# Layer 1's queries and values as 15 block products per half of the tokens, in a two-layer attention kernel

## The chip, the cores and the metric

The kernel runs on one core of a Trainium2 chip. Its time is the device time of one execution in microseconds (us), and the time before is the median of three executions. One further execution was taken with the hardware profiler; the profile's rows and the trace come from it. The engines are TensorE (PE in the profile; its weight loads are PEld), VectorE (DVE), ScalarE (ACT), GpSimd (POOL) and SyncE (SP). Each takes the instructions of its own queue in order. SP issues most transfers, POOL and ScalarE issue some.

## What is computed

Eight images of 32 x 32 = 1024 tokens with 384 channels go through two layers in float32. Layer 0 is group norm, attention with 6 heads and relative positions, and a projection, added to the input. Layer 1 is attention with one causal head of 384 channels, added to its input; a feed-forward block with binarized weights follows it. Cut to what matters here:

```python
def _L1_attn_ref(x, Wq, Wk, Wv):
    q = jnp.einsum('btc,ch->bth', x, Wq)
    k = jnp.einsum('btc,ch->bth', x, Wk)
    v = jnp.einsum('btc,ch->bth', x, Wv)
    scores = jnp.einsum('bth,bsh->bts', q, k) * scale
    ...
    return jnp.einsum('bts,bsh->bth', softmax(scores), v)

x = x + _L0_conv_ref(_gn(x), ...)
t = _to_tokens(x)
t = t + _L1_attn_ref(_ln_t(t), L1_attn_Wq, L1_attn_Wk, L1_attn_Wv)
t = t + _L1_ffn_ref(_ln_t(t), L1_ffn_W1, L1_ffn_b1, L1_ffn_W2, L1_ffn_b2)
```

The feed-forward block's output is zero for all but the first five images, so the kernel leaves it out for images 5, 6 and 7.

## The kernel before

The images are worked one after the other, in the order 5, 0, 1, 2, 3, 4, 6, 7 (`ORDER`). A tile is at most 128 partitions wide; the 384 channels are three blocks of 128. Tiles are taken from pools of buffers: 12 pages of 128 x 1024, 10 larger `image` (or `flat`) buffers, and the 8 banks of PSUM, which `o_tile` hands out. A scheduler orders the instructions of each engine when the program is built; `tc.issue_after(ins)`, and `behind_of`, which calls it, put the instructions that the block creates on `ins`'s engine behind `ins` in that engine's queue. `last_ended` is the VectorE instruction that such a block last stood behind, `in_turn` does the same for TensorE.

Layer 0 (`layer0`, `attend0_fast`) makes queries by plain products (L629), and keys and values by a scheme that was there before (L555): the three input blocks and the three output blocks of the weights, with the 1024 tokens in two halves of 512, make a product of a 2 x 3 by a 3 x 3 block matrix, which takes 18 block products plainly and 15 by this scheme. The scheme works on forms: sums and differences of the input's blocks (`image_forms`, L527) and of the weights' blocks (`weight_forms`, L172, made once by POOL into `wf`). `PROD_ORDER` (L40) lists the 15 products with the PSUM bank (A to F) in which each accumulates and the name under which ScalarE copies the bank's running value to SBUF (`keep`, L581). Between some copies VectorE takes differences (`PROD_COMBINE`, L606), and it ends each of the six output blocks with one sum of a bank and a kept value (`finish`, L614; the order that comes out is D, E, F, C, B, A). A bank that is copied midway takes further products after the copy.

In the scores loop of layer 0 a pair of heads p and a half of the queries take 16 us; VectorE adds up the probabilities (L862) and POOL multiplies the output by the reciprocals (L912). During pair 1 the tables `r` of the last pair are placed by 16 transfers, 8 issued by SP and 8 by POOL (`place`, L743), and `residual` (L820) loads the input again and adds a bias on POOL (L823).

Layer 1 (`attention1`, L981) begins with the projection of layer 0's output (L472, `more`), layer norm of the first half of the tokens (`layer_norm_T`: statistics, normalising to xn at L462, transposing by TensorE at L398 and copying to lnT by ScalarE at L399), and goes on with queries (L989) and values (L472, copied at L993) for each half of 512 tokens. The keys are not made: scores are formed with the product of Wq and Wk^T, which `multiply_out` (L378) computes once and keeps in SBUF as `wqk`. Then `between` runs the group norm of the next image (`group_norm_T`, L411): VectorE takes statistics (L418) and aggregates them (L419), TensorE averages over the groups with a one-column product (L422), VectorE goes on with the mean (L424 to L427), and a second such product follows (L430). The scores of layer 1 (L1030), their exponentials (L1039) and the values (L1045) stand behind it in `attend1_fast`. At the very start, `turn_biases` (L164) transposes bias rows on TensorE, VectorE copies the result (L167), and `join_biases` (L362) multiplies part of it on TensorE.

Of the kernel before, what the change touches and what calls it, by code (L numbers as in the profile page):

```python
# [11 lines left out]
F32 = mybir.dt.float32  # L12
# [7 lines left out]
P = 128  # L20
# [71 lines left out]
def conv_attn_hybrid(  # L92
# [35 lines left out]
    wproj_sb, wv_sb = (tile_of(n, [P, NC, C]) for n in ("wproj_sb", "wv_sb"))  # L128
# [11 lines left out]
    def load_weights(pools):  # L140
# [16 lines left out]
        nc.sync.dma_start(out=wv_sb, in_=wv.rearrange("(k p) o -> p k o", p=P))  # L157
# [6 lines left out]
    def turn_biases(pools, rows):  # L164
        ps = pools.o_tile("biases")
        nc.tensor.transpose(ps[:, : 3 * NC + NM], rows, ident[: 3 * NC + NM, : 3 * NC + NM])
        nc.vector.tensor_copy(biases, ps[:, : 3 * NC + NM])  # L167
# [4 lines left out]
    def weight_forms(pools, eng, raw, s):  # L172
# [3 lines left out]
        room = pools.page(f"wsum_{s}")  # L176
# [5 lines left out]
        def f(r):  # L182
            return wf[:, r, s - 1, :]
# [101 lines left out]
    w2s = store.tile([P, NM * C], F32R, name="w2s")  # L285

    def load_plain():
        nc.sync.dma_start(out=wqkv_sb, in_=qkv_w.rearrange("(p k) o -> p k o", k=NC))
    wqk = const.tile([P, NC, C], F32, name="wqk")
# [88 lines left out]
    def multiply_out(pools, wqT_sb, wkT_sb):  # L378

        for m in range(NC):  # L380
# [5 lines left out]
            with tc.issue_after(first_root[0]):  # L386
                nc.scalar.mul(wqk[:, m, :], ps[:, :C], C**-0.5)

    def stages(pools):
# [137 lines left out]
        def image_forms(b, xT, eng):  # L527

            rooms = [pools.page(f"xf_{b}_{i}") for i in range(len(X_MADE) // 2)]
            made = {r: rooms[i // 2][:, ts(i % 2, 512)] for i, r in enumerate(X_MADE)}  # L530

            def x(k, n):
                return xT[:, k, ts(n, 512)]

            def add(r, a, b, op=ALU.add):
                eng.tensor_tensor(made[r], a, b, op)  # L536
# [17 lines left out]

        class ProductSet:  # L555

            def __init__(self, b, s, forms):
                self.name, self.s, self.forms = f"{b}_{s}", s, forms
# [4 lines left out]
            def kept(self, name):  # L563
                if name not in self.part:
                    pair = next(pair for pair in PROD_PAGES if name in pair)
                    room = pools.page(f"u_{self.name}_{pair[0]}")
                    self.part.update({n: room[:, ts(i, 512)] for i, n in enumerate(pair)})
                return self.part[name]

            def multiply(self, ps, r, start):  # L570
                x, w = self.forms[r], wf[:, r, self.s - 1, :]
                if self.s == 1:
                    in_turn(ps, w, x, start=start, stop=True, skip_group_check=True)
                    return
                keys = x.rearrange("p (g i n) -> p g n i", g=2, n=2)
                for j in range(4):
                    in_turn(
                        ps[:, ts(j, P)], keys[:, j // 2, j % 2], w, start=start and j == 0, stop=True, skip_group_check=True
                    )
# [779 lines left out]
```

## Time and profile before

| what | us |
|---|---|
| executions, median of three (lowest to highest) | 2315.85 (2315.0 to 2317.25) |
| the profiled execution | 2316.79 |
| its span, from the first to the last instruction | 2314.8 |
| TensorE busy | 2295.1 |
| layer 1's queries, L989, 18 matmuls per image | 127.5 busy |
| layer 1's values, L472, 24 matmuls per image | 126.5 busy |
| VectorE, ScalarE, POOL busy | 1526.6, 1099.2, 413.4 |

The profiled execution is one execution, 0.9 us above the median. The mean granted clock of TensorE was 0.998 of full speed over the span. A matmul in float32 leaves two records in the profile, so "x12" stands for six matmuls; its records overlap with those of the next one, so that the distance from start to start, and not the duration of one record, is what it costs. "Idle before" is the time in which an engine had nothing to do just before an instruction, with what ended it behind the arrow. A line number is that of the helper that creates the instruction: L525 holds layer 0's queries, position tables and block products alike, and L472 both the projection of layer 0 and the values of layer 1. Three rows by form, for the operations that the change multiplies: line, engine, operation, tiles, shapes and count; busy time and mean duration; idle time before.

```
L606 DVE TENSOR_TENSOR f_u_n<-f_u_n,f_u_m 128x512 f32<-128x512 f32 x32 | 22.1, 691 | 17.4
L586 ACT COPY f_u_n<-f_pr_A 128x512 f32<-128x512 f32 x48 | 28.2, 587 | 42.6
L536 POOL TENSOR_TENSOR f_xf<-f_gnT 128x512 f32<-128x512 f32 x28 | 35.5, 1279 | 503.0
```

### The profile page before, as it was taken

To read this page: it belongs to the slowest core of one execution; us is meant where nothing else is said; L and a number is where in the kernel's file an instruction comes from. 1 tells how busy PE (TensorE), PEld (TensorE's weight loads), DVE (VectorE), ACT (ScalarE), POOL (GpSimd) and SP (SyncE) were. 2 spreads that over 40 slices of the span, in tenths; PEclk is the share of its full clock that TensorE was granted. 3 is DMA by queue.
4 is the path that set the end of the run, shared out by engine and by line. 5 is a ranking of instruction groups with operands and counts; after the bars stand their busy time and mean duration, and the time that the engine had idled before them with its cause. 6 is when DMAs were issued, how large, how long until landed. Compare 5 with 4: busy or idle time off the path is not lost.

```text
span 2314.8 us, 27729 instructions
## 1 busy us (share of the span) xinstructions
PE 2295.1 (99%) x9971; PEld 1317.8 (57%) x9971; DVE 1526.6 (66%) x2432; ACT 1099.2 (47%) x1876; POOL 413.4 (18%) x520
## 2 busy tenths in 40 slices
PE   8999999999999999999999999999999999999998
PEld 4545554568645577545685455874457754555454
DVE  5885578575887348884468864579734788527851
ACT  4642266137663257642467522766324765116611
POOL 4320222030140201311102302013020131021300
PEclk9999999999999999999999999999999999999999
DMA  6530561040730115510318102074002362017100
GB/s 164 155 116 1 152 139 56 38 162 28 148 99 28 62 48 119 129 54 1 110 40 187 47 28 109 28 142 105 28 28 82 97 140 64 1 51 159 37 1 29
DMA packets 153980, 185.82 MB, mean 80 GB/s; under 512 B 110901, under 2 KB 123562, under 8 KB 151018
## 3 DMA queue, kind: packets, MB, share of 16 engines
q1 hardware_dynamic: 135456, 113.28, 20.2%
q0 software_dynamic: 17184, 69.22, 9.5%
q8 instruction: 82, 1.34, 0.2%
q10 hardware_dynamic: 1194, 1.45, 0.2%
q14 instruction: 64, 0.52, 0.1%
HBM read 83.24 MB, written 50.33 MB: 58 GB/s over the span
## 4 chain that ended last, share of the span: by engine, by line
PE 97%; DVE 1%; ACT 1%; DMA 0%; issue 0%; POOL 0%; ACTq 0%; DVEq 0%
PE f_s L844 15%; PE f_av L870 14%; PE f_s L1030 8%; PE f_av L1045 8%; PE f_y L1155 7%; PE f_y L1205 7%; PE f_pj L472 5%; PE f_v L472 5%; PE f_q L989 5%; PE f_qk L525 5%; PE f_pr_A L525 4%; PE f_s L848 4%; PE f_pr_B L525 3%; PE f_rel L525 2%; PE f_pt L398 1%; PE f_pr_D L525 1%
## 5 line engine op out<-in xcount | busy, mean ns | idle before, releaser
L855 ACT ACTIVATE f_pr<-f_s 128x512 f32<-128x512 f32 x768 | 413.2, 595 | 41.2 <-PE f_s L848 34.7
L844 PE MATMUL f_s<-f_q,f_k 64*128 64x512 f32 x1536 | 399.0, 595 | 0.0
L862 DVE TENSOR_TENSOR f_sum<-f_sum,f_pr 128x1024 f32<-128x1024 f32 x288 | 363.3, 1262 | 23.5 <-ACT f_pr L855 1.4
L870 PE MATMUL f_av<-f_pr,f_v 128*64 128x512 f32 x1536 | 339.3, 594 | 0.0
L848 PE MATMUL f_s<-f_r,unit 64*128 64x512 f32 x768 | 307.4, 792 | 0.0
L870 PEld LDWEIGHTS f_av<-f_pr,f_v 128*64 128x64 f32 x1536 | 106.2, 137 | 196.4 <-issue 191.9
L844 PEld LDWEIGHTS f_s<-f_q,f_k 64*128 64x128 f32 x1536 | 145.6, 186 | 124.0 <-issue 64.6
L1030 PE MATMUL f_s<-f_q,f_lnT 128*128 128x512 f32 (+3 forms) x576 | 195.9, 488 | 0.0
L1045 PE MATMUL f_av<-f_v,f_pr 128*128 128x385 f32 x576 | 195.3, 486 | 0.0
L1039 ACT ACTIVATE f_pr<-f_s 128x512 f32<-128x512 f32 (+3 forms) x96 | 46.9, 491 | 279.6 <-DVE f_s L1035 233.9
L743 POOL DMA_DIRECT2D f_r<-f_far x192 | 102.2, 535 | 401.2 <-DVE f_far L737 189.5
L1045 PEld LDWEIGHTS f_av<-f_v,f_pr 128*128 128x128 f32 x576 | 108.2, 190 | 77.2 <-issue 11.5
L1030 PEld LDWEIGHTS f_s<-f_q,f_lnT 128*128 128x128 f32 x576 | 102.0, 190 | 77.8 <-issue 53.8
L1166 DVE TENSOR_REDUCE am<-f_h 128x1 f32<-128x1024 f32 (+2 forms) x80 | 71.6, 947 | 96.3 <-ACT f_h L1159 96.3
L1159 ACT ACTIVATE f_h<-f_y,biases 128x256 f32<-128x256 f32 x240 | 100.9, 472 | 67.4 <-PE f_y L1155 67.4
L525 PE MATMUL f_qk<-f_gnT,wq_sb 128*128 128x512 f32 x288 | 127.8, 595 | 0.0
L989 PE MATMUL f_q<-f_lnT,wqk 128*128 128x512 f32 x288 | 127.5, 592 | 0.0
L472 PE MATMUL f_pj<-wproj_sb,f_oT 128*128 128x384 f32 x384 | 127.3, 488 | 0.0
L1205 PE MATMUL f_y<-f_w2a,f_hilo 128*128 128x384 f32 x640 | 127.1, 341 | 0.2
L472 PE MATMUL f_v<-wv_sb,f_lnT 128*128 128x384 f32 x384 | 126.5, 486 | 0.0
L848 PEld LDWEIGHTS f_s<-f_r,unit 64*128 64x128 f32 x768 | 75.0, 187 | 90.0 <-issue 89.8
L536 POOL TENSOR_TENSOR f_xf<-f_gnT 128x512 f32<-128x512 f32 x28 | 35.5, 1279 | 503.0 <-DVE f_gnT L435 503.0
(217 smaller groups left out, 3519.2 us busy)
## 6 DMA issues: line engine op xcount, KB each, us to landing
f_far<-f_far SPq DMA_DIRECT2D x48, 512.0 KB, 4.6
f_r<-f_far SPq DMA_DIRECT2D x192, 128.0 KB, 2.9
f_r<-f_far POOLq DMA_DIRECT2D x192, 128.0 KB, 4.5
f_far<-f_far SPq DMA_DIRECT2D x192, 64.0 KB, 4.7
f_x<-in_x SPq DMA_DIRECT2D x32, 384.0 KB, 7.2
f_gnT<-in_xT SPq DMA_DIRECT2D x21, 512.0 KB, 4.5
f_w1a<-w1s POOLq DMA_DIRECT2D x5, 1536.0 KB, 6.8
f_w2a<-w2s POOLq DMA_DIRECT2D x5, 1536.0 KB, 9.2
```

The costliest lines, as they stand in the source:

```text
L472: nc.tensor.matmul(ps[:, :C], xT[:, k, ts(j, P)], w[:, k, cols], start=(k == 0), stop=(k == NC - 1))
L525: last_product[0] = nc.tensor.matmul(*args, **kw).ins
L844: nc.tensor.matmul(sc[par], k[rows[par], p, ts(c, P)], q[rows[par], p, ts(half, 512)], start=True, stop=False)
L848: last_matmul[0] = nc.tensor.matmul(sc[par], unit[rows[par], c // 2 % 2].rearrange("i h w -> i (h w)"), r(2 * (c // 4) + c % 2, p)[rows[pa ...
L855: last_exp[0] = nc.scalar.activation(pr[:, ts(par, 512)], sc[par], AF.Exp).ins
L862: adds.append(nc.vector.tensor_tensor(total, total, pr, ALU.add).ins)
L870: last_matmul[0] = nc.tensor.matmul(av[ts(par, HD), :], v[:, c, ts(2 * p + par, HD)], pr[:, ts(par, 512)], start=(c == 0), stop=(c == NJ - 1),
L989: nc.tensor.matmul(ps, wqk[:, k, ts(m, P)], xT[:, half, k, :], start=(k == 0), stop=(k == NC - 1))
L1030: nc.tensor.matmul(sc[:, lo:], xT[:, c // 4, k, ts(c % 4, P)], q[:, half, k, lo:], start=(k == 0), stop=(k == NC - 1),)
L1045: nc.tensor.matmul(av[:, : C + 1], prs[c][:, ts(j - c, P)], v[:, c, :], start=(c == 0), stop=(c == j))
L1155: nc.tensor.matmul(ps, w1k[i // 2][:, ts(m, P)], xs[i % 2][:, half, i // 2, :], start=(i == 0), stop=(i == 2 * NC - 1))
L1205: nc.tensor.matmul(ps[:, :C], h, w, start=(i == 0), stop=(i == len(products) - 1))
```

## The change

The queries and the values of layer 1 are made by the same 15-product scheme, once per half of the tokens, with the half's 512 tokens in two blocks of 256. A set of products is thus 15 matmuls of 256 columns for queries, and 15 x 2 matmuls of 128 tokens by 128 channels for values; there are four sets per image.

- `sum_forms` generalises `image_forms` to a width and to an engine for each form. In layer 1, POOL makes forms 5, 6 and 12 and VectorE the others, from lnT.
- `ProductSet` takes the weights' forms, a width, the token tiles, whether a bias is added, and the engine of the differences, which is POOL for the sets of layer 1. The ten copies by ScalarE and the six final sums by VectorE (to q and v) are as in layer 0.
- The queries of half 0 come ahead of the layer norm of half 1, then the forms of half 1, the values of half 0, and the queries and values of half 1.
- The weights' forms of layer 1, `w1f`, are made once by POOL, in the first image (image 5), after `residual`: 42 operations on 128 x 128 blocks. For this `wqk` is written to memory by SP at the start and read back with Wv (SP also) at that time. SP no longer loads Wv at the start. `w1f` takes the place of `wqk` and `wv_sb` in SBUF.
- The group norm of the next image is put behind the last final sum (`behind_of(last_ended[0])`).
- ScalarE in place of VectorE copies the transposed biases.

The core of the diff:

```diff
-        nc.vector.tensor_copy(biases, ps[:, : 3 * NC + NM])
+        nc.scalar.copy(biases, ps[:, : 3 * NC + NM])
...
+    def layer1_forms(pools):
+        room = pools.flat("raw_1")
+        plain = [room[:, ts(i, NC * C)] for i in range(2)]
+        nc.sync.dma_start(out=plain[0], in_=wqk_kept)
+        nc.sync.dma_start(out=plain[1].rearrange("p (k o) -> p k o", k=NC), in_=wv.rearrange("(k p) o -> p k o", p=P))
+        for s in range(2):
+            weight_forms(pools, nc.gpsimd, plain[s].rearrange("p (k o) -> p k o", k=NC), s, w1f)
...
-                nc.scalar.mul(wqk[:, m, :], ps[:, :C], C**-0.5)
+                nc.scalar.mul(made[:, m, :], ps[:, :C], C**-0.5)
+        nc.sync.dma_start(out=wqk_kept, in_=made.rearrange("p k c -> p (k c)"))
...
+                            made = self.eng.tensor_tensor(self.part[dst], self.part[dst], self.part[other], ALU.subtract)
+                        if self.eng is nc.vector:
+                            last_ended[0] = made.ins
...
                 if (p, half) == (1, 0):
                     xt = residual()
+                    if b == ORDER[0]:
+                        layer1_forms(pools)
...
+            def forms_of(half):
+                return sum_forms(
+                    f"1_{b}_{half}", lambda k, n: xT[:, half, k, ts(n, 256)], 256,
+                    lambda r: nc.gpsimd if r in (5, 6, 12) else nc.vector,
+                )
+
+            def products(half, forms):
+
+                def put_queries(ps, kept, p, n, op):
+                    return nc.vector.tensor_tensor(q[:, half, p, ts(n, 256)], ps, kept, op).ins
+
+                def put_values(ps, kept, p, n, op):
+                    ps, kept = (t.rearrange("t (j c) -> t j c", j=2) for t in (ps, kept))
+                    j = 4 * half + 2 * n
+                    return nc.vector.tensor_tensor(v[:, j : j + 2, ts(p, P)], ps, kept, op).ins
+
+                ProductSet(f"1q_{b}_{half}", forms, w1f[:, :, 0, :], 256, eng=nc.gpsimd).run(N_PROD, put_queries)
+                yield
+                of_v = ProductSet(
+                    f"1v_{b}_{half}", forms, w1f[:, :, 1, :], 256, lambda x: [x[:, ts(j, P)] for j in range(2)], eng=nc.gpsimd
+                )
+                of_v.run(N_PROD, put_values)
...
-            for m in range(2):
-                queries(0, m)
-            layer_norm_T(xt, xT, 1, f"1_{b}")
-            queries(0, 2)
-            for j in range(4):
-                values(j)
-            for m in range(NC):
-                queries(1, m)
-            for j in range(4, NJ):
-                values(j)
+            if pools.fast:
+                first = products(0, forms_of(0))
+                next(first)
+                layer_norm_T(xt, xT, 1, f"1_{b}")
+                forms = forms_of(1)
+                next(first, None)
+                for _ in products(1, forms):
+                    pass
...
                     if b in AFTER:
                         norm = group_norm_T(AFTER[b])
-                        made = next(norm)
+                        with behind_of(last_ended[0]):
+                            made = next(norm)
                         yield made
```

## The prediction

> **What bounds the kernel now.** I read the page first: busy shares, then the chain that ended last.
>
> ```profile
> span 2314.8 us, 27729 instructions
> PE 2295.1 (99%) x9971; PEld 1317.8 (57%) x9971; DVE 1526.6 (66%) x2432; ACT 1099.2 (47%) x1876; POOL 413.4 (18%) x520
> PE 97%; DVE 1%; ACT 1%; DMA 0%; issue 0%; POOL 0%; ACTq 0%; DVEq 0%
> ```
>
> TensorE carries 97% of the chain, so a TensorE microsecond saved is a microsecond gained, and each wait that the change puts before TensorE costs its full length. Next the chain in order of time, at the second image: here are layer 1's queries (L989) and values (L472).
>
> ```profile
> 425.44 5.15 PE f_q L989 x12
> 431.90 2.58 PE f_q L989 x6
> 434.47 7.74 PE f_v L472 x24
> 442.21 7.72 PE f_q L989 x18
> 449.94 7.74 PE f_v L472 x24
> 463.17 8.49 PE f_s L1030 x24
> ```
>
> Start, length, count; a float32 matmul leaves two records. So a 512-wide matmul takes 5.15/6 = 0.858 us and a 384-wide one 7.74/12 = 0.645. Then the timeline, for what the new code resembles and for what surrounds it.
>
> ```profile
> 297.65 1.10 PE L525 MATMUL f_pr_A<-wf,f_xf 128*128 128x128 f32 x8
> 298.58 1.10 PE L525 MATMUL f_pr_B<-wf,f_xf 128*128 128x128 f32 x8
> ...
> 311.43 0.69 DVE L769 TENSOR_TENSOR f_v<-f_pr_C,f_u_n 128x512 f32<-128x512 f32 x1
> 312.04 0.68 DVE L769 TENSOR_TENSOR f_v<-f_pr_B,f_u_m 128x512 f32<-128x512 f32 x1
> ...
> 422.55 1.63 ACT L399 COPY f_lnT<-f_pt 128x384 f32<-128x384 f32 x4 [4.32 <-PE f_pt L398]
> 425.27 5.31 PE L989 MATMUL f_q<-f_lnT,wqk 128*128 128x512 f32 x12
> 429.69 3.06 DVE L418 BATCH_NORM_STATS2 gst<-f_gnT 128x6 f32<-128x512 f32 x5
> 457.52 0.28 PE L422 MATMUL f_gmean<-gmv,over_group 128*128 128x1 f32 x2
> 457.66 5.40 PE L1030 MATMUL f_s<-f_q,f_lnT 128*128 128x512 f32 x12
> ```
>
> To see: layer 0's values by the same scheme start a product (four 128-wide matmuls) every 0.935 us, 0.234 a matmul; VectorE takes the next image's statistics (L418) at 429.69, long before TensorE wants their mean (L422) at 457.52.
>
> **What is removed and added on TensorE.** Removed per image: 18 matmuls of 0.858 = 15.45 and 24 of 0.645 = 15.48, together 30.93. Added: queries, 2 halves x 15 products 256 wide; at half of 0.858 that is 30 x 0.429 = 12.87. No row shows a 256-wide product alone; the last line of the chain above holds 4992 columns in 8.49 us where 0.858 per 512 gives 8.37, so its three 256-wide ones cost at most 0.04 more each, and 30 at most 14.1. Values: 60 matmuls x 0.234 = 14.04. So 4.0 saved (at least 2.8), 32 in eight images.
>
> **The start of a half.** The first product wants form 5, two subtractions on POOL; the second wants form 11, after VectorE's forms 2, 0, 4, 1, 7 and the residual addition that the built order puts between them. lnT's copies end at 424.18, TensorE is free at 425.27. VectorE: 128x512 takes 0.69, 128x1024 1.26, so 256 about 0.41, near 0.47 where one waits for the other; five forms end at 426.3, the addition (0.56) at 426.9, form 11 at 427.3. The row of forms made with POOL busy (512 wide, 0.905 instead of 0.69) says up to 0.6 each, 428.1. TensorE has 0.43 us of product 1 in that time: a wait of 1.2 to 2.6, taken 1.9. The second half's forms lie beside the first half's values and cost nothing; without that cover, another 2.
>
> **Inside a set.** Products accumulate in a bank of which ScalarE copies the running value in between; the last product waits for the copy made two products earlier. The copy starts 0.30 after the product's issue (0.20 for values), takes 0.41 at 256 (between 0.587 at 512 and 0.498 at 384), and TensorE goes on 0.06 later: 0.77 where 0.43 passes, 0.67 where 0.47 passes. Before, at 512, 0.95 against 0.86 showed as a 0.09 slip. Three sets slip, 0.2 + 0.34 + 0.2 = 0.74. The rest of the 40 copies (16.4 us an image) and 24 final sums (some 9 us) has room beside TensorE, as the windows view shows: stretch, length, then busy time (count) of TensorE, weight loads, VectorE, ScalarE, POOL.
>
> ```profile
> 424.00:463.00 39.00, 39.00 (x117) 20.58 (x115) 17.19 (x40) 4.97 (x10) 0.00 (x0) 1.00 0.01 3
> ```
>
> In the first queries' set more goes wrong: the four normalised tiles (xn) of half 1 stand on VectorE behind that set's final sums, and those wait for ScalarE's copies and POOL's subtractions (0.7 at 256, between 0.41 at 128 and 1.24 at 512). From product 2 I step: sum D at 4.05, xn 4 by 4.9, E 5.35, F, xn 5, xn 6 by 6.95, C, B, A, xn 7 by 8.55; so half 1's last transposes end at 9.0, where 14 x 0.43 + 1.23 of transposes would end at 7.25. Taken 1.75 (0.5 if the sums slip past, 2.5 with slow POOL).
>
> **The end of the stage, the largest term.** The edit at the group norm queues L418 on VectorE behind the last final sum of the second values, but the built order of TensorE still has the mean product (L422's) directly behind the last product and ahead of layer 1's scores. TensorE takes its queue in order, so all scores wait. From T, the last product's issue: the copy it waited for ended at T - 0.53 (0.47 of product, 0.06 of waking), POOL's subtraction ends at T + 0.2, sums C, B, A (spaced 0.34, half of the 0.61 between the lines of L769 above, the last lasting 0.42) end at T + 1.3; six statistics at 3.06/5 = 0.61 each end at T + 5.0, the aggregate (0.32) at T + 5.3, and the scores follow 0.3 later instead of 0.14 after T: 5.45 us (4.8 with quick sums, 6.2 with a POOL that waits). Queued behind the mean product are the scores, for which ScalarE's exponentials wait. This strikes the seven images that have a successor.
>
> **The clock.** Idle time may cost twice.
>
> ```profile
> 15.00:16.00 1.00, 0.20 (x2) 1.00 0.92 307
> 17.00:18.00 1.00, 0.65 (x1) 0.50 0.98 273
> 20.50:21.00 0.50, 0.50 (x3) 1.00 0.01 3
> ```
>
> These are stretches of the windows view for TensorE: stretch, length, busy (count), clock, then transfers. After a gap of 2.15 us (with little work ahead of it) the granted clock was 0.50 from about 17.0 to 20.3; six matmul records, three matmuls, took 3.69 us there instead of 1.93, a loss of 1.76. I charge 1.7 (0 to 2.5) for each of the seven long waits, the full price of that row since the wait is longer.
> [...]
>
> **Once per run.** w1f's forms are 42 POOL operations in image 5's attention, after the residual additions that end at 106.0; 35 of them and two 2.3 us multiplications now stand ahead of the seven transfers of r for the last pair, issued from 121.24 before and needed at 134.1. POOL's 128x128 form took 0.88 beside a busy VectorE and 0.45 beside an idle one. At 0.7: 106 + 24.5 + 4.8 = 135.3, with 0.53 an issue and 4.5 to land some 4 us late (0 at 0.45, 10 at 0.88). Taken 4. SP's two added loads (wqk back, wv; 576 KB, 5 to 7 us) stand behind x's and ahead of r's there, which were first issued at 113.09: hidden unless a buffer for them is late; uncovered, 7 us once, inside that 10. The wqk store is queued ahead of SP's first table transfer, at 34.97; its data are there at 16.4: nothing. The bias copy: ScalarE gets to it at about 16.4 where VectorE ran it at 17.12, -0.7 (0 to -2.5, if the low clock is escaped).
>
> **Sum.** An image with a successor: -4.0 + 1.9 + 1.75 + 0.74 + 5.45 + 1.7 = +7.5; seven, +52.8. The last: +0.4. Once: +4 - 0.7. Together +56.5 on 2316.79, the profiled execution (span 2314.8 and 2.0 around it), 0.9 above the median of the runs shown, 2315.85: 2372 for the median.
>
> **Rivals.**
> The full clock: the waits are there but the clock never falls: 2372 - 12 = 2360. For it: the only fall in the trace is at the start, beside other things; against: these waits are longer. 0.2.
> POOL in image 5 as the bound: r's transfers 10 us late, and the multiplications queued behind the forms hold pages that the probabilities want, another 8: 2386. For it: POOL's doubled durations there; against: it happens once, with 28 us between the residual and the need. 0.1.
> Not slower, by the statistics being ready: if VectorE is done with L418 when the last product ends, the mean product passes in 0.14 as before, no clock is lost, and the set waits stay at the low ends (1.2 + 0.5 + 0.4): 8 x -1.9 + 3.3 on 2315.85 = 2304. For it: VectorE is busy only 17.2 of the 39 us from 424 to 463, so the work has room. Against it: the built order of VectorE, six statistics behind the last sum. It decides once the end wait is below about 1.5 us. 0.08. Its half way, waits that eat up just the 4 us, gives 2316; 0.03.
>
> **Numbers.** Forecast 0.59, the full clock 0.2, POOL 0.1, not slower 0.11. The low ends together (waits 0.7, 1.25 and 0.65 smaller in seven images, full clock, POOL's 4 gone) give 2338, so the range begins at 2336. Upwards, POOL's rival with the clock at 2.5 (+5.6) gives 2392, and a saving of 3.4 instead of 4.0 4 more: 2396; all high ends at once I leave out. Faster by over 0.2% (4.6 us, about what a measurement of this kernel can tell from none) 0.08, within it 0.03, slower 0.89.
>
> **What would show it.** TensorE idle some 5 us ahead of L422's successor in seven images, ended by VectorE's aggregate; granted clock near 0.5 in the first 3 us of the scores; four sets of 6.5 to 7.3 us; idle of 1 to 2 us ahead of the first set's second product and among half 1's transposes. If the statistics start before the last sum, or the scores stand ahead of the mean product, the forecast is wrong; if the idle is there and the clock full, only by 12.

## The result, and the profile after

The changed kernel took 2399.12 us (median of four executions, 2393.63 to 2401.06) against 2316.55 of the kernel before (four, 2315.0 to 2317.31): a ratio of 1.0351, 95% interval 1.0338 to 1.0363. It is slower, by 3 us more than the range allowed for. The profiled execution has a span of 2399.2 us, 84.4 more than before. Its page, in the places shown of before (span; busy time of the engines; shares of the chain that ended last):

```profile
span 2399.2 us, 30264 instructions
PE 2309.8 (96%) x10739; PEld 1406.4 (59%) x10739; DVE 1625.6 (68%) x2639; ACT 1210.0 (50%) x2181; POOL 592.7 (25%) x754
PE 89%; DVE 6%; POOL 2%; DMA 1%; issue 1%; ACT 1%; SPq 0%; ACTq 0%; DVEq 0%; POOLq 0%
```

TensorE fell from 97% of the chain to 89%, and VectorE and POOL took the difference: TensorE now waits for them. The view of waits says where (who waited, line, for whom; us in total, times, longest):

```profile
PE f_gmean L437 <- DVE gmv L434: 36.3, 7, 5.2
PE f_pr_1q_B L540 <- DVE f_xf L549: 16.9, 8, 2.1
PE f_pt L413 <- DVE f_xn L477: 6.7, 8, 0.8
...
PE f_pr_1q_A L540 <- POOL f_xf L549: 5.6, 8, 0.7
PE f_s L869 <- issue: 3.8, 1, 3.8
```

Lines have moved: the mean product is now L437, the aggregate L434, the products L540, the forms L549, xn L477, the scores of layer 1 L1081. The first line is the end wait of seven images; the second and the fifth are the start of the first query set in eight; the third is half 1's transposes; the last ("issue": nothing that the profile shows) stands in image 5 at the first product on r, seven of whose transfers POOL now issues from 134.07 instead of 121.24. TensorE's timeline at the second image, whose stretch in the kernel before the prediction showed:

```profile
437.06 1.47 PE L413 MATMUL f_pt<-ident,f_xn 128*128 128x128 f32 x12
438.37 2.10 PE L487 MATMUL f_pj<-wproj_sb,f_oT 128*128 128x384 f32 x6
441.17 0.70 PE L540 MATMUL f_pr_1q_A<-f_xf,w1f 128*128 128x256 f32 x2 [0.70 <-POOL f_xf L549]
443.98 0.70 PE L540 MATMUL f_pr_1q_B<-f_xf,w1f 128*128 128x256 f32 x2 [2.11 <-DVE f_xf L549]
444.52 0.71 PE L540 MATMUL f_pr_1q_C<-f_xf,w1f 128*128 128x256 f32 x2
445.02 1.06 PE L540 MATMUL f_pr_1q_A<-f_xf,w1f 128*128 128x256 f32 x2
445.88 1.06 PE L540 MATMUL f_pr_1q_B<-f_xf,w1f 128*128 128x256 f32 x2
...
474.94 0.71 PE L540 MATMUL f_pr_1v_A<-w1f,f_xf 128*128 128x128 f32 x4
480.84 0.59 PE L437 MATMUL f_gmean<-gmv,over_group 128*128 128x1 f32 x2 [5.19 <-DVE gmv L434]
481.29 7.64 PE L1081 MATMUL f_s<-f_q,f_lnT 128*128 128x512 f32 x12
```

Read the starts. Products 4 to 7 of the first set come 0.85 us apart, where later sets have 0.43; the first twelve records of the scores, six matmuls, last 7.64 us, where before they took 5.40. The windows view names the cause (stretch, length, busy time and count of five engines, then TensorE's granted clock, the DMA share and GB/s); the first three lines are the first set, the others the scores:

```profile
444.00:445.00 1.00, 1.00 (x4) 0.86 (x5) 0.93 (x4) 0.28 (x1) 0.00 (x0) 0.93 0.00 0
446.00:447.00 1.00, 1.00 (x4) 0.81 (x3) 0.00 (x0) 0.40 (x2) 0.00 (x0) 0.50 0.00 0
449.00:450.00 1.00, 1.00 (x6) 0.89 (x5) 0.23 (x1) 0.51 (x2) 0.73 (x1) 1.00 0.00 0
484.00:485.00 1.00, 1.00 (x3) 0.48 (x2) 0.00 (x0) 0.00 (x0) 0.00 (x0) 0.50 0.00 0
486.00:487.00 1.00, 1.00 (x3) 0.38 (x2) 0.61 (x4) 0.28 (x1) 0.00 (x0) 1.00 0.00 0
```

The clock is 0.50 after both waits. The long one was forecast to do this; the pair of short ones (0.70 and 2.11 us, with one product between) was not.

### The profile page after: what moved, and what is told of

It reads as the page before. It is cut to its first block, busy times and chain, and to the rows that moved or that the text cites. A ratio compares the mean times of both kernels' runs of the same rounds, so it can differ in the third digit from the quotient of the medians.

```text
span 2399.2 us, 30264 instructions
## 1 busy us (share of the span) xinstructions
PE 2309.8 (96%) x10739; PEld 1406.4 (59%) x10739; DVE 1625.6 (68%) x2639; ACT 1210.0 (50%) x2181; POOL 592.7 (25%) x754
## 4 chain that ended last, share of the span: by engine, by line
PE 89%; DVE 6%; POOL 2%; DMA 1%; issue 1%; ACT 1%; SPq 0%; ACTq 0%; DVEq 0%; POOLq 0%
PE f_s L865 13%; PE f_av L891 12%; PE f_s L1081 8%; PE f_av L1096 8%; PE f_y L1256 7%; PE f_y L1206 7%; PE f_qk L540 5%; PE f_pj L487 5%; PE f_pr_A L540 4%; PE f_s L869 3%; PE f_pr_B L540 3%; PE f_rel L540 2%; PE f_pr_1v_A L540 2%; PE f_pr_1q_A L540 1%; DVE f_xf L549 1%; PE f_pr_1v_B L540 1%
## 5 line engine op out<-in xcount | busy, mean ns | idle before, releaser
L1081 PE MATMUL f_s<-f_q,f_lnT 128*128 128x512 f32 (+3 forms) x576 | 211.7, 517 | 0.0
L1081 PEld LDWEIGHTS f_s<-f_q,f_lnT 128*128 128x128 f32 x576 | 108.0, 201 | 86.7 <-issue 63.3
L881 DVE TENSOR_TENSOR f_sum<-f_pr,f_pr 128x1024 f32<-128x1024 f32 x48 | 64.8, 1349 | 97.9 <-ACT f_pr L876 87.3
L540 PE MATMUL f_qk<-f_gnT,wq_sb 128*128 128x512 f32 x288 | 127.8, 595 | 0.0
L936 ACT COPY f_oT<-f_av 128x512 f32<-128x512 f32 x40 | 23.4, 586 | 191.9 <-PE f_av L891 191.9
```

Of the source, the lines that this page charges most:

```text
L540: last_product[0] = nc.tensor.matmul(*args, **kw).ins
L1081: nc.tensor.matmul(sc[:, lo:], xT[:, c // 4, k, ts(c % 4, P)], q[:, half, k, lo:], start=(k == 0), stop=(k == NC - 1),)
```

## The experiments

Each kernel is the changed one with the edit shown, except the last, which starts from the kernel before. Times are medians, with the ratio to the kernel before and its interval; that ratio is not the quotient of the two medians. Line numbers shift a little from kernel to kernel.

### The end of the stage

Statistics left free (e1):

```diff
-                        with behind_of(last_ended[0]):
-                            made = next(norm)
+                        made = next(norm)
```

> The changed kernel with the group norm of the next image no longer put behind the last final sum; all else as changed. In its built order VectorE takes three of the six statistics among the forms of half 1 and three ahead of the first values' sums, and the mean product stands ahead of the last product of the second values. My theory: the end wait (5.2 us of idleness, 5.7 from the last product to the scores) and the half clock behind it (2.3 us) are both due to the place of the statistics, so seven times 8.0 = 56 us go: 2343 us, the first scores back at about 5.2 us for six matmuls. Rival one, the wait comes back elsewhere: the statistics (6 x 0.6 us) now delay the first values' sums and with them the second half by up to 2 to 3.6 us an image: 2360 to 2370. Rival two, the scores are slow for another reason than the wait before them: 2359, with the scores still at 7.4 us.

Measured: 2345.91 us, 1.0129 [1.0112, 1.0146]. The end wait is gone and the scores' clock with it (the 512-wide score matmuls are back from 146.5 to 132.0 us busy). One new wait stands in its place, as the first rival had it, but smaller:

```profile
PE f_pr_1q_B L540 <- DVE f_xf L549: 16.9, 8, 2.1
PE f_pt L413 <- DVE f_xn L477: 6.7, 8, 0.8
PE f_pr_1q_C L540 <- DVE f_v L1033: 6.7, 7, 1.4
```

The third product of half 1's queries waits for a PSUM bank, which half 0's sums (L1033), now behind three statistics, release late: 6.7 us over seven images. So of the 55 us at the end, 7 came back here.

Mean product behind the first scores, statistics where they were (e5):

```diff
-            room = between()
-            got = next(room, None)
-            (attend1_fast if pools.fast else attend1_general)(xt, b, q, xT, v, room, lambda: start(got))
+            def room():
+                for got in between():
+                    found.append(got)
+                    yield
...
+                xt, b, q, xT, v, room(), lambda: start(found[0] if found else None)
```

> The changed kernel with the statistics still behind the last final sum, but the group norm's steps each taken one block of scores later, so that the mean product stands on TensorE behind the first two blocks of scores. Nothing else moves. My theory: the wait is one of TensorE's queue order, scores standing behind a product that wants the statistics; with the scores ahead, seven times 8.0 = 56 us go, 2343 us, although VectorE does the same in the same order. Rival: the last final sums themselves are late (they end 1.4 us after the last product), so the scores find the bank or q not ready and wait 1 to 1.5 us, or the group norm, 5 us later, is late for the next image: 2350 to 2355.

Measured: 2365.21 us, 1.0202 [1.0185, 1.0219], worse than both forecasts. The scores ahead of the mean product run at full speed, but the view of waits still has

```profile
PE f_gmean L437 <- DVE gmv L434: 18.5, 7, 4.8
```

VectorE's timeline at the image worked fourth shows why:

```profile
1113.70 0.30 DVE L1093 TENSOR_TENSOR f_s<-f_s,maskT 128x128 f32<-128x128 f32 x1 [1.12 <-PE f_s L1088]
1113.91 3.65 DVE L433 BATCH_NORM_STATS2 gst<-f_gnT 128x6 f32<-128x512 f32 x6
```

Taking the step later put the statistics behind the mask addition of the first scores (L1093), which waits for TensorE. The mean product went later, and so did what it waits for. Moving the waiter alone is not the mend. The clock was not spared either: between the mean product and the second one-column product, 4.59 us passed in three images and 6.28 to 6.54 in four, two behind waits of 4.6 and 4.8 us and two of the five behind 1.81 us. The scores there, in the image worked second and in the one worked fourth:

```profile
485.71 6.70 PE L1088 MATMUL f_s<-f_q,f_lnT 128*128 128x384 f32 x12
...
1118.27 4.76 PE L1088 MATMUL f_s<-f_q,f_lnT 128*128 128x384 f32 x12
```

Statistics between the sets (f1), behind the last sum of half 0's values, and the mean product behind the last product of half 1's queries:

```diff
             nc.vector.bn_aggr(mv, st.rearrange("p k a s -> p (k a s)"))
+            if steps:
+                yield
...
                 next(first, None)
-                for _ in products(1, forms):
-                    pass
+                room = between()
+                next(room, None)
+                second = products(1, forms)
+                next(second)
+                got = next(room, None)
+                next(second, None)
```

> The changed kernel with the statistics of the next image behind the last sum of half 0's values, where VectorE idles while half 1's queries run, and the mean product on TensorE behind the last product of half 1's queries. All else as changed. My theory: the end wait is only a matter of where these seven VectorE operations and the one-column product stand in two queues. The statistics end about 467.5 on the scale of the second image, the mean product is reached at 468.5, so no wait takes its place: the end wait with its clock goes, seven times 7.9 = 55 us, and the first kernel's loss at the PSUM bank (0.9 us an image when the statistics were left free) does not come: 2344 us. [...] Rival: half 1's sums are pushed back by the statistics and the queries of half 1 meet full banks or late copies: 0.5 to 1.5 us an image, 2348 to 2356.

Measured: 2341.72 us, 1.0107 [1.009, 1.0124]. Neither the end wait nor the wait for a bank is in the profile; the start's waits are there to the last tenth. The place of seven VectorE operations and one product in two queues is what the end cost.

### The clock by itself

Matmuls that nothing reads, three of 512 columns ahead of the first set and five ahead of the mean product (e2):

```diff
+        def keep_warm(name, n):
+            ps = pools.o_tile(name)
+            for _ in range(n):
+                in_turn(ps, ident, w1f.rearrange("p r s o -> p (r s o)")[:, :512], start=True, stop=True)
...
+                keep_warm(f"warm0_{b}", 3)
...
+                            keep_warm(f"warm1_{b}", 5)
```

> The changed kernel with matmuls added that nothing reads: three of 512 columns ahead of the first query set's first product, five between the last product of the second values and the mean product, in the images where those waits are. They fill 2.6 of the 2.8 us of idleness at the start and 4.3 of the 5.2 us at the end; the waits themselves stay. My theory, that the granted clock falls because TensorE is idle, and that this alone makes products 3 to 8 of the first set and the first six scores slow: the scores return from 7.4 to 5.2 us (seven times 2.2 = 15) and the first set gains 1.8 us (eight times = 14): 2399 - 29 = 2370 us. Rival, the slow matmuls come from something else (VectorE's and POOL's traffic, or the operands): no change or up to 3 us more, 2399 to 2402. Half way, only the long wait at the end lowers the clock: 2384.

Measured: 2375.11 us, 1.0253 [1.0236, 1.027]: 24 us less than the changed kernel, by more work on TensorE. The mean clock of the span rose from 0.981 to 0.998. The scores came back whole: in the timeline the mean product still comes late, and the 12 records behind it take 5.40 us again.

```profile
476.89 0.38 PE L437 MATMUL f_gmean<-gmv,over_group 128*128 128x1 f32 x2 [0.89 <-DVE gmv L434]
477.14 5.40 PE L1088 MATMUL f_s<-f_q,f_lnT 128*128 128x512 f32 x12
```

From the second product of the first set to the start of the last transposes it was 9.57 us in every image, where the changed kernel had 8.70 to 11.74: the fall of the clock is gone, and 0.9 an image was given back (7 us in all; the forecast missed by 5), 0.6 of this at product 4, because product 1 stood behind the added matmuls and its copy was late.

### The start of the first set

All forms on VectorE (e3):

```diff
-                    lambda r: nc.gpsimd if r in (5, 6, 12) else nc.vector,
+                    lambda r: nc.vector,
```

> The changed kernel with all ten forms of layer 1 made by VectorE, none by POOL. In its built order VectorE makes seven operations and the residual addition up to form 11, where it made six with POOL beside it. My theory, that the start wait (3.25 us from the end of the projections to the second product, beside the product itself) was mis-sized because VectorE and POOL slow each other: each form takes 0.43 us instead of 0.8 to 0.94, form 11 is there at 442.8 instead of 444.0 on the scale of the second image, so the start loses about 2 instead of 3.25 us: eight times 1.2 = 10 us, and if the shorter wait leaves the clock up another 14: 2375 to 2389 us. Rival, the forms are slow whatever POOL does (their operands or their chain of dependences): seven at 0.85 make the wait 0.9 us longer: 2406.

Measured: 2375.74 us, 1.0253 [1.0236, 1.027], the favourable end of the forecast. One of VectorE's forms now takes 0.42 us, where it took 0.83 to 0.96 beside POOL. The wait for POOL is gone, that for form 11 is 11.5 us instead of 16.9 (1.4 an image), and the stretch after it took 8.76 us in all eight images: after 1.4 us of idleness the clock never fell.

The start mended in three ways, first try (f2): all forms on VectorE, `layer_norm_T` of half 0 after six projections instead of seven, and half 1's xn made ahead of the first set:

```diff
-            for j in range(7):
+            for j in range(6):
...
-                first = products(0, forms_of(0))
-                next(first)
-                layer_norm_T(xt, xT, 1, f"1_{b}")
+                forms = forms_of(0)
+                turn = layer_norm_T(xt, xT, 1, f"1_{b}", wait=True)
+                first = products(0, forms)
+                next(first)
+                turn()
```

> The changed kernel with the start of the first query set mended and the end left as it is: all forms on VectorE, the layer norm of half 0 after six projections instead of seven (so that two projections run on TensorE while lnT is copied and the forms are made), and half 1's normalised tiles ahead of the first set's final sums on VectorE. My theory, that the start costs 3.25 us of waits, 1.9 us at half clock (15.4 over eight images) and 1.6 us of late transposes: xn is 0.8 us late for its transposes at the earlier place, the rest goes, so 8 x (2.45 + 1.6) + 15.4 = 48 us: 2351 us. Rival: VectorE, now with all forms and four normalised tiles ahead of the sums, becomes late for the banks or for half 1's forms: 1 to 2 us an image back, 2360 to 2367.

Measured: 2375.43 us, 1.0251 [1.0234, 1.0268]; neither theory. The old waits are gone, but each image has 2.0 us ahead of its fourth product. ScalarE's timeline (from the run with all mends below, which has the same start):

```profile
426.89 0.87 ACT L414 COPY f_lnT<-f_pt 128x384 f32<-128x384 f32 x2 [0.32 <-PE f_pt L413]
433.89 0.20 ACT L466 ACTIVATE lsd<-lsd 128x4 f32<-128x4 f32 x1 [6.13 <-DVE lsd L465]
434.00 0.35 ACT L613 COPY f_u_1q<-f_pr_1q_A 128x256 f32<-128x256 f32 x1
```

The square root of half 1's variance (L466) now stands ahead of the first set's copies and comes at 433.89, when VectorE has the statistics; the copies of products 1 to 3, which TensorE began at 430.96, 431.39 and 431.82, stand behind it, and product 4 must not overwrite bank A before its copy. With the forms and the projections as in f2, but half 1's layer norm between product 5 and product 6 (g2):

```diff
+                of_q.run(5, put_queries)
+                yield
+                of_q.run(N_PROD - of_q.at)
                 yield
...
+                turn = layer_norm_T(xt, xT, 1, f"1_{b}", wait=True)
+                next(first)
+                turn()
```

> The start alone mended, with the square root placed as in the run beside it; the end of the stage and image 5 as in the changed kernel. My theory: the first try at this (2375 us) kept 2.0 us in each image because ScalarE's queue had the square root of half 1 ahead of the first copy; without it 2375 - 16 = 2359 us, so that the start with its clock is worth 40 of the 83 us. Rival: half 1's normalised tiles, now later, miss the transposes again (0.8 us an image): 2366.

Measured: 2355.73 us, 1.0171 [1.0155, 1.0186], 43 us below the changed kernel. Of the start's waits, 0.3 us an image is left in the view of waits, at the first transposes.

### Image 5's weight forms

The 42 forms on POOL after the last pair's first scores (f3, without the third added line), then behind POOL's last multiplication as well (g3):

```diff
-                    if b == ORDER[0]:
-                        layer1_forms(pools)
+                if (p, half) == (2, 0) and b == ORDER[0]:
+                    with behind_of(scaled.ins):
+                        layer1_forms(pools)
```

> The changed kernel with the 42 weight forms of layer 1 made after the first scores of the last pair in image 5 instead of after the residual, so behind the transfers of r for that pair in POOL's queue. My theory: the 3.8 us that TensorE waited in image 5 for r's last transfers, about 1.2 us of half clock behind it and the wait of 1.0 for a sum go: 2399 - 5 = 2394 us, and no such wait shows. Rival: the forms are late for layer 1's first products, which begin 50 us after that point with 42 forms of 0.5 to 0.9 us on POOL: up to 10 us slower at image 5's first query set, 2405.

> The changed kernel with the 42 weight forms alone moved, behind the last multiplication by POOL in image 5's attention. My theory: neither r's transfers nor that multiplication is late any more, so both waits of image 5 in the changed kernel (3.8 and 1.0 us) go, with 1.3 us of half clock: 2399 - 6 = 2393 us. [...] Rival: the forms, now begun about 140 and on POOL at up to 0.9 us each beside a busy VectorE, end later than 185, and the first query set of image 5 waits for them: 2400 to 2405.

Measured: 2399.01 us (2387.32 to 2404.7), 1.0336 [1.0309, 1.0363], and 2395.79 us (2395.1 to 2403.4), 1.0354 [1.0339, 1.037]: no gain that can be told. In both the wait for r's transfers is gone, and TensorE waits for the last sum of probabilities instead, 5.7 and 10.6 us. The wait had moved each time, and neither forecast knew what carried it. The run h1, below, takes it away.

### All mends together

f4 has f1, f2 and f3 in one kernel; g1 has f1, g2 and g3; g4 is g1 with the last product of three sets behind the first matmul of what follows:

```diff
-                of_q.run(N_PROD - of_q.at)
+                of_q.run(N_PROD - of_q.at - half)
...
-                of_v.run(N_PROD, put_values)
+                of_v.run(1, put_values)
+                if half:
+                    of_q.run(1)
+                of_v.run(N_PROD - 2)
+                yield
+                of_v.run(1)
```

> All three mends of the runs beside it at once. My theory: what is left is TensorE's saving of 4.6 us an image, less 0.8 us of slips where a 15th product waits for ScalarE's copy and 0.8 us for late normalised tiles, and the start of the kernel 2 us earlier: 2316.7 - 8 x 3.0 - 2 = 2290 us, 1.1% faster than before. Rival one, the waits return elsewhere, since VectorE now carries every form and the statistics between half 1's sums: 2300 to 2315. Rival two, the price of the scheme itself (copies, sums, POOL's subtractions) is what TensorE cannot hide, whatever the order: 2320 or more.

> The kernel with all three mends, two of them placed anew: the statistics, square root and normalised tiles of half 1 come between the fifth and the sixth product of the first query set (so that ScalarE's square root, which waits for the last statistics, no longer stands ahead of the set's first copies), and the 42 weight forms stand behind the last of POOL's multiplications in image 5, not only behind r's transfers. My theory: in the run with all mends, 2.0 us at the fourth product of each first set (16 in all) and 5.7 in image 5 were left, both put there by my own placing. Without them 2319 - 16 - 5.7 = 2297 us, 0.9% faster than the kernel before: the scheme's saving on TensorE (4.6 us an image) then shows, less 0.8 of slips and about 0.8 at the transposes. Rival: VectorE, which now carries all forms, four normalised tiles and six statistics in the space of the stage, is late for the next thing in turn and another 1 to 2 us an image come back: 2305 to 2315.

> As the run with all mends placed anew, with one more change: the last product of half 0's values, half 1's queries and half 1's values stands behind the first matmul of what follows it. My theory: this last product waits 0.2 us for ScalarE's copy made two products earlier; with another matmul between, three such slips per image go, 8 x 0.6 = 5 us less than the run beside it, about 2292. Rival: the final sums that hang on the last product come 0.4 us later, and the next set's banks or the first scores wait for them: no difference, or 1 to 3 us more.

Measured: f4 2319.04 us, 1.0006 [0.9997, 1.0016]; g1 2303.63, 0.9946 [0.9932, 0.9959]; g4 2298.62, 0.9921 [0.9908, 0.9935]. f4 has the 2.0 us of ScalarE's square root in each image (15.9) and 5.7 in image 5. g1 is 7 us above its forecast, because image 5 had 10.6 instead of none. g4 gains the 5 us forecast for it.

In g4 VectorE's additions of the last pair's probabilities in image 5, and the product of TensorE that marks the time in both kernels, read

```profile
152.22 6.96 DVE L892 TENSOR_TENSOR f_sum<-f_pr,f_pr 128x1024 f32<-128x1024 f32 x1 [4.37 <-POOL w1f L189]
159.29 9.05 DVE L894 TENSOR_TENSOR f_sum<-f_sum,f_pr 128x1024 f32<-128x1024 f32 x4
156.50 0.29 PE L920 MATMUL f_den<-few,fold 128*64 128x16 f32 x4
```

The first waits for a POOL form and then takes 6.96 us, where such an addition takes 1.23; four more take 9.05. The forms' scratch sums lie in a page (`wsum`); h1 puts them into the unused end of the buffer that holds the raw weights:

```diff
-        room = pools.page("wsum")
+        room = pools.page("wsum") if room is None else room
...
+                pools, nc.gpsimd, plain[s].rearrange("p (k o) -> p k o", k=NC), s, w1f, room[:, 2 * NC * C : 2 * NC * C + 2 * P]
```

> The run with all mends and interleaved last products, with one change: the scratch sums of the weight forms (two 128 x 128 blocks, held while POOL works through 42 operations) lie in the unused end of the buffer with the raw weights instead of in a page. My theory: the 10.6 us that TensorE still waited in image 5 came from this page: VectorE's sum of the last pair's probabilities wants the next page in turn, which the scratch held until POOL was done at 167, so the wait goes: 2298.6 - 10.6 = 2288 us. Rival: the sum waits for POOL's multiplication or for POOL's traffic beside it, not for a page: no change, 2298.

Measured: 2285.35 us, 0.9862 [0.9847, 0.9878], 1.4% faster than the kernel before. The same rows, and then TensorE's waits and the chain of this kernel:

```profile
153.15 1.45 DVE L894 TENSOR_TENSOR f_sum<-f_pr,f_pr 128x1024 f32<-128x1024 f32 x1 [3.59 <-ACT f_pr L889]
154.71 5.49 DVE L896 TENSOR_TENSOR f_sum<-f_sum,f_pr 128x1024 f32<-128x1024 f32 x4
158.49 0.29 PE L922 MATMUL f_den<-few,fold 128*64 128x16 f32 x4
```

```profile
PE f_wqk L399 <- DMA f_wqkT<-in_wkT: 6.5, 1, 6.5
PE f_pt L415 <- DVE f_xn L481: 2.5, 8, 0.3
PE f_bad L278 <- DVE worst L276: 1.9, 1, 1.9
PE f_pb L380 <- ACT biases L170: 1.5, 1, 1.5
PE f_av L1132 <- ACT f_pr L1126: 0.7, 1, 0.7
PE f_den L922 <- DVE few L915: 0.6, 1, 0.6
```

```profile
span 2286.1 us, 30217 instructions
PE 96%; DVE 2%; DMA 1%; POOL 1%; issue 0%; ACTq 0%; ACT 0%; DVEq 0%; POOLq 0%
```

The place of the scratch sums carried the wait: with them elsewhere it falls from 10.6 to 0.6, although POOL works through its 42 forms in the same stretch. The number of the forecast came, but mostly not by its theory, a wait for the page until 167. Measured from TensorE's product, which comes 1.99 us later in h1, the first addition starts only 1.1 us later in g4 than in h1 (152.22 and 153.15). The other 9 us are the five additions, 16.1 us from the first start to the last end in g4 and 7.0 in h1; in h1 POOL is the slow one instead, with up to 1.5 us for a form that takes 0.45. Why another place for two small blocks decides which engine is slowed is not shown. Behind the 10.6 us the first 36 records of the projection took 14.75 us instead of 11.88, at a granted clock of 0.50 at first: 2.9 more, which is why h1 gained 13 us where 10.6 were forecast.

### The bias copy alone

```diff
-        nc.vector.tensor_copy(biases, ps[:, : 3 * NC + NM])
+        nc.scalar.copy(biases, ps[:, : 3 * NC + NM])
```

> The kernel before with one part of the change alone: ScalarE instead of VectorE copies the transposed biases. My theory: in the changed kernel the first query matmul of layer 0 started at 18.76 instead of 20.87, 2.1 us earlier, because the wait ahead of it fell from 2.15 to 1.0 us and the half clock behind it mostly did not come. If the copy alone does that, 2316.6 - 2.1 = 2314.5 us, just visible. Rival: part of it comes from the load of Wv, which the change takes out of the start: 1 us or less, 2315.6 or no difference.

Measured: 2314.1 us against 2316.94, 0.999 [0.9981, 0.9999]. The windows of the stretch that the prediction showed of before:

```profile
16.00:17.00 1.00, 0.49 (x2) 0.36 (x3) 1.00 (x2) 0.87 (x5) 0.54 (x1) 1.00 1.10 336
17.00:18.00 1.00, 1.00 (x5) 0.60 (x4) 0.96 (x2) 0.00 (x0) 1.00 (x2) 1.00 0.98 218
18.00:19.00 1.00, 1.00 (x5) 0.50 (x4) 0.05 (x1) 0.00 (x0) 1.00 (x3) 1.00 1.02 327
20.00:21.00 1.00, 1.00 (x3) 0.41 (x3) 1.00 (x2) 0.00 (x0) 1.00 (x3) 1.00 0.16 60
```

The clock stays at 1.00 where it was 0.50 from about 17 to 20.3. The wait ahead of the bias product fell from 2.15 to 1.32 us and the first query matmul came at 18.55 instead of 20.87: 0.8 us less of waiting and 1.5 us of half clock escaped. That is as much as the changed kernel gained there: its first query matmul starts at 18.59 in the timeline, not at 18.76, which is the end of the product before it in the view of the chain. The load of Wv, which this kernel still has, plays no visible part.

## Why the prediction was right in kind and short in size

The terms, us in eight images (seven for those of the end). Measured values are from the second image's start-to-start distances unless a count over all images is given.

| step | forecast | measured |
|---|---|---|
| TensorE's work saved | 8 x -4.0 = -32.0 | 8 x -4.6 = -36.7 |
| start of the first set | 8 x 1.9 = 15.2 | 8 x 3.25 = 26.0 |
| half clock in the first set | 0 | 15.4 |
| half 1's transposes late | 8 x 1.75 = 14.0 | 8 x 1.64 = 13.1 |
| 15th product behind its copy | 8 x 0.74 = 5.9 | 8 x 0.84 = 6.7 |
| end wait | 7 x 5.45 = 38.2 | 7 x 5.68 = 39.8 |
| half clock in the scores | 7 x 1.7 = 11.9 | 15.6 |
| image 5 | 4 | 4.8 + 1.5 = 6.3 |
| start of the kernel | -0.7 | -2.3 |
| sum | 56.5 | 83.9 of 84.4 |

How the measured ones come out: products 0.4315 and 0.4467 apart, 30 of each, 26.35 in place of 30.93; the first product 0.87 and the second 2.38 later than back to back; first sets from the second product to the start of the last transposes 8.70 us at full clock, and over the eight images 15.4 more; at full clock 9.09 from the second product to the values, where 14 products and 1.31 of transposes take 7.35, with 0.1 of the difference put down to the 15th product; scores 481.29 - 474.94 - 0.53 = 5.82 behind the place where the last product ends, 0.14 before; the first 12 score records 52.2 us in seven images in place of 7 x 5.23; in image 5 waits of 3.8 and 1.0, and behind the first of them 9.90 us of scores in place of 8.36; the first query matmul at 18.59 in place of 20.87. The 84.4 are the difference of the two profiled spans.

**Two steps failed, both at the start of a half.** The first is the clock: the prediction charged it "for each of the seven long waits" alone, although its own row showed it falling after 2.15 us at the start of the kernel, and it forecast waits of 1.2 to 2.6 us in eight places more. This is 15.4 of the 27 us by which the two sums differ, and the run with added matmuls shows it to be the clock. The same omission cost 1.5 in image 5, behind the wait for r. The second, 10.8 of the 27, is the start wait's size, 3.25 instead of 1.9, above its own high end: the forms beside POOL took 0.83 to 0.96 us, twice the 0.41 to 0.47 taken, where a row 30% longer for 512 columns had set the bound; and POOL's two operations for form 5 made the first product wait too, which was not in the sum. e3 shows that the forms are quick without POOL, 0.42 us each.

**The end of the stage was right**, in place, releaser and size. e1 and f1 show that both its parts hang on the place of the statistics: 36.3 us of waits and the scores' clock went with it, and the later wait that e1 opened was for banks. The price of the clock there, 2.2 instead of 1.7, was taken from a row that followed a shorter wait; it was inside the given 0 to 2.5, whose high end was the author's estimate.

**Transposes, slips and image 5.** The first two held within 1 us each over the run, and the saving came out 4.7 us better: a 128-wide matmul of the values took 0.223, not 0.234. In image 5 the wait for r was 3.8 us, as the 4 forecast; the 1.0 for a late sum and the 1.5 of half clock were not in the sum. The view was too narrow as well: the forms were seen as a queue on POOL that a busy VectorE slows (0.88 us a form against 0.45), and that VectorE's additions slow down beside them (16.1 us for the five in g4, 7.0 in h1) was found only when moving the forms did not help.

**The rivals.** The full clock is refuted by the windows view and by e2. POOL as the bound would have cost 18 us in image 5, 10 for r and 8 for the pages; all of image 5 cost 6.3. "Not slower" needed the end wait below 1.5 us; with that wait taken out (f1) the kernel is still 1.1% slower, so this rival also lacked the start.

**Where the expected gain went.** It exists: with the waits out (h1) the kernel is 31.6 us faster than before, 2.8 of them by the bias copy (0.2 to 4.4 by the interval of its ratio). In the changed kernel 37 us of TensorE's work were saved as well, and 123 us of waits, slips and low clock were put in front of it.

## What to carry to other kernels

When TensorE is the chain, a scheme that saves it matmuls and gives the other engines forms, copies and sums has to be placed operation by operation: here the same arithmetic ran from 3.5% slower to 1.4% faster by queue positions, one engine's choice and one scratch buffer. Charge the clock to every wait of about 1.8 us or more ahead of matmuls (here it fell behind 2 of 5 waits of 1.8 us, behind 32 of 48 pairs of 0.70 and 2.11 us, and behind each of 5.2 us), as a range that includes nothing, and not only to the longest. If a moved piece of work leaves the time as it was, look for what it slows beside it in its new place and for where its scratch lies before moving it again, and for the queue (ScalarE's square root, VectorE's mask addition) in which the new place has put something else behind a wait.

## What the runs showed of the hardware

The fall of the clock depended here on something besides the wait. Six kernels (the changed one, e1, e5, f1, f3, g3) have the same pair of waits, 0.70 and 2.11 us, in eight images each. The stretch after it was lengthened by 0 in 16 of the 48 images, by 1.4 to 1.7 us in 22 and by 2.9 to 3.05 in 10. Two images from e1, one after the other, with the same waits; the products of the first come 0.54 and then 0.43 us apart, those of the second 1.02 and then 0.85:

```profile
1065.19 0.70 PE L540 MATMUL f_pr_1q_B<-f_xf,w1f 128*128 128x256 f32 x2 [2.12 <-DVE f_xf L549]
1065.73 0.59 PE L540 MATMUL f_pr_1q_C<-f_xf,w1f 128*128 128x256 f32 x2
...
1378.90 1.22 PE L540 MATMUL f_pr_1q_B<-f_xf,w1f 128*128 128x256 f32 x2 [2.11 <-DVE f_xf L549]
1379.92 1.06 PE L540 MATMUL f_pr_1q_C<-f_xf,w1f 128*128 128x256 f32 x2
```

A single wait of 1.4 us (e3) never lowered the clock in eight images, one of 1.8 us (e5) did in 2 of 5, one of 2.0 us (f2, f4) in 1 of 16, the 5.2 us in every image that has it, for 1.8 to 2.5 us of loss in the changed kernel and 1.5 to 3.0 in the others that have it (e3, f2, f3, g2, g3). What else decides it, no run here shows. The least idleness ahead of a fall was 1.8 us alone, or 2.8 us with a product of 0.43 between. The spread also makes the time uncertain where such waits are: the profiled runs of f3 and g3, 2402.8 and 2393.1 us of span, have 16.8 and 4.8 us of it.

VectorE and POOL slowed each other, and not evenly: additions of two SBUF operands at 128 x 256 took 0.42 us alone (e3) and 0.83 to 0.96 beside POOL (the changed kernel), POOL's 128 x 128 forms 0.45 alone (the kernel before) and up to 2.2 beside VectorE (in the changed kernel's image 5), and in g1, g3 and g4 a VectorE addition of 128 x 1024 took 6.96 to 6.98 us, instead of 1.23, while POOL's forms ran at 0.45. Which of the two gives way, and when, these runs do not settle.
